# Graph attention layer: other tiles for the transferred sums, group ends on every second step, earlier loads of the row factors, a fifth special tile

## The chip, the cores and the metric

The kernel runs on one core of a Trainium2 chip. The metric is the device time of one execution in microseconds (us). Before the change it is 2991.66 us, the median of 3 runs (2991.22 to 2992.32).

The engines are called as the profile calls them: PE multiplies matrices (PEld loads its weights), DVE is the vector engine, ACT the engine for activations, POOL the general one, SP issues most transfers (DMAs). Each takes its instructions in the order in which the program lists them.

## What is computed

Two layers of a graph network over 4096 nodes with 512 features. Layer 0 is not touched. Layer 1, cut to what matters:

```python
h = jnp.maximum(_layernorm(x, axis=-1), 0.0)
data1 = (h @ W.T + b).reshape(N, H, D)            # N 4096, H 8 heads, D 64
src = jnp.einsum('nhd,xhd->nh', data1, src_proj)
trg = jnp.einsum('nhd,xhd->nh', data1, trg_proj)
e = src.T[:, :, None] + trg.T[:, None, :]
e = jnp.where(e >= 0, e, 0.01 * e)
e = e + adj[None, :, :]
scores = jax.nn.softmax(e, axis=-1)
out = jnp.einsum('hnm,hmd->hnd', scores, data1.transpose(1, 0, 2))
x = x + out.transpose(1, 0, 2).reshape(N, H * D)
```

For every head and every node n, 4096 weights over m are made, summed (the divisor) and used to average the rows of data1.

## The kernel before

Layer 0 takes the first 1760 us or so. Then layer 1 runs in **8 groups**: 4 blocks of 1024 nodes n, times 2 halves of the heads, 4 heads each. In a group there are **32 tiles**, one for each 128 nodes m. A step of the loop at the end of the layer is one tile of one group; 256 steps in all.

One tile of a group holds, for each of the 4 heads k, the unnormalized weights `pr{k}`: 128 nodes m on the partitions, 1024 nodes n along them. It comes about like this:

- `load` (3 steps ahead): SP fetches the tile of the transposed adjacency, `e`, 512 KB (three buffers).
- `exps` (1 ahead): ACT takes exp of it into PSUM, `ex`. `last_exps` (2 ahead): ACT takes exp with a bias, `e3`, for head 3, in which a factor of the row is already contained. `relus` (2 ahead): ACT makes `rl` for head 0 from the row factor `z0`.
- `weigh` (1 ahead): DVE multiplies for each head in the order 3, 0, 1, 2 the larger of a row factor `z{k}` and a column factor by `ex` or `e3` (L756; L753 for head 0). These are four DVE instructions on 128 x 1024 a tile.
- On the **special tiles**, BY_LOG, head 0 goes without DVE: `logs` (5 ahead) has ACT make `lg` from the row term `u` (L731), a transfer issued by POOL adds the adjacency to it on the way (L732), and `relus` takes one exp of the sum (L739).
- `gather` (0 ahead): PE multiplies the weights with the rows of data1 (`pv`, L788). For fp32 the profile shows two instructions for each matmul in the source: 32 a tile. Each writes 32 of the 128 rows of a PSUM tile; the four blocks of 32 rows belong to two **sides**, r = 0 (the first 64 rows) and r = 1.

The divisors are sums over all m of the same weights. Heads 1 and 2 go through PE in each tile (`dn<-pr,d_m`, 8 instructions, all four blocks). Head 3 is added up by POOL (`acc3`, L765) and enters PE once, at the last tile. For **head 0** there are two ways:

- on the tiles of **BY_DMA** a transfer issued by POOL adds the tile to one of two accumulators `acc00` and `acc01` in turn (L770, L772); both enter PE at the last tile;
- on all others, `by_pe`, PE sums the tile itself (`dn<-pr,zo`, L802): 4 instructions on the two blocks of one side. `side` changes with each such tile, and a tile begins its matmuls with the side that is not behind.

Before, BY_DMA is 2, 3, 4, 6, 7, 8, 10, 11, 12, 14, 15, 16, 18, 19, 20, 22, 23, 24, 26 (19 tiles), and by_pe 0, 1, 5, 9, 13, 17, 21, 25, 27, 28, 29, 30, 31 (13 tiles). The special tiles are 17, 21, 25, 29.

The **end of a group**, `finish`, runs inside the next group, one piece behind each step's gather: copy and transposes of the divisors (the small matmuls at L827), their reciprocal `rd`, and then for each of 8 pieces of 128 nodes two transposes on PE (`turn`, L843, 128 x 128, in the trace a pair of instructions of 0.44 us together), four scaled copies on ACT (`o`), for each two pieces an accumulating transfer that adds x1 (POOL, L870) and a store (SP, L873), three calls behind the accumulation. The transposes so lie behind tiles 2 to 9. Group 0 carries no end of a group but `tables`, which makes the row factors of the other groups, with transposes behind tiles 2, 4 and 5.

The **row factors** `z0` to `z3` of the next group (L691) are loaded at tiles 20, 22, 24, 26, `u` at tile 28. There are two sets of buffers for z, used by groups in turn; one for `u`. All loads and stores named "SP" are in one queue, in the order of the program. `finish_last` closes the last group, with ACT and DVE sharing 8 transposed pieces.

At the last tile, dn gets the sums of heads 1 and 2, head 0 of the tile (side 0), head 3 of the tile (side 1), acc01 (side 0), acc00 (side 0) and acc3 (side 1), in this order.

Of the kernel before, what the change touches and what calls it, by code (L numbers as in the profile page):

```python
# [8 lines left out]
FP = mybir.dt.float32  # L9
# [6 lines left out]
P = 128  # L16
# [12 lines left out]
def kernel(  # L29
# [15 lines left out]
    nc = tc.nc  # L45
    N, F = x.shape
    H, D = 8, 64
    HG, WL = 4, 1024
    WT = WL // P
    NT = N // P  # L50
# [49 lines left out]
    with tc.tile_pool(name="w0", bufs=1) as wp, tc.tile_pool(name="a0", bufs=2) as ap_, tc.tile_pool(  # L100
        name="a0s", bufs=8
# [15 lines left out]
        lg = wp.tile([P, NT], FP, name="lg")  # L117
# [514 lines left out]
    HV = WL // BL  # L632
    JT = BL // P
    Q = P // 4
    BY_LOG = (17, 21, 25, 29)
    BY_DMA = [m for m in range(2, NT - 5) if m % 4 != 1]

    with tc.tile_pool(name="p", bufs=2) as prp, tc.tile_pool(name="rl", bufs=2) as rlp, tc.tile_pool(
        name="io1", bufs=3
    ) as iop, tc.tile_pool(name="s1", bufs=1) as sp, tc.tile_pool(name="za", bufs=1) as zp0, tc.tile_pool(name="e3", bufs=2) as e3p, tc.tile_pool(  # L640
        name="zb", bufs=1
    ) as zp1, tc.tile_pool(name="e", bufs=3) as ep, tc.tile_pool(name="ac", bufs=2) as acp, tc.tile_pool(
        name="os", bufs=1
    ) as osp, tc.tile_pool(name="u", bufs=1) as usp, tc.tile_pool(
        name="p_x", bufs=1, space=PSUM
    ) as p_x, tc.tile_pool(name="p_v", bufs=1, space=PSUM) as p_v, tc.tile_pool(
        name="p_t1", bufs=1, space=PSUM
# [9 lines left out]
        def tables():  # L657

            for h in range(H):
                nc.scalar.activation(s_n[:, h, :], s_n[:, h, :], AF.Relu, bias=tmb[:, h:h + 1])  # L660
                if h % 3 == 2:
                    yield
            pz = p_t.tile([P, 2, P], FP, name="pt")
            for g in range(H // HG):
                nc.tensor.transpose(pz[:NT, g, :], s_n[:, g * HG, :], ident)
            yield
            ut = sp.tile([NT, 2, P], FP, name="ut")
            nc.scalar.copy(ut, pz[:NT])
            nc.gpsimd.dma_start(u_d.rearrange("g t p -> t g p"), ut)
            nc.scalar.activation(s_n, s_n, AF.Exp, scale=-(1.0 - SLOPE))  # L670
            yield
            s_f = s_n.rearrange("p h t -> p (h t)")
            for c in range(H * NT // P):
                pz = p_t.tile([P, P], FP, name="pt")
                nc.tensor.transpose(pz, s_f[:, c * P:(c + 1) * P], ident)
                yield
                zt = sp.tile([P, P], FP, name="zt", bufs=2)
                nc.scalar.copy(zt, pz)
                nc.gpsimd.dma_start(z_d[c * P:(c + 1) * P, :], zt)
            yield  # L680
# [12 lines left out]
        def load(i, m):  # L693
            b, g = groups[i]
            e = ep.tile([P, WL], FP, name="e")
            nc.sync.dma_start(e, adj_t[m * P:(m + 1) * P, b * WL:(b + 1) * WL])
            ra[i, m] = e
            if i + 1 < len(groups) and m == 28:
                us[i + 1] = usp.tile([P, WL], FP, name="u")
                b, g = groups[i + 1]  # L700
                nc.sync.dma_start(us[i + 1], row_bcast(u_d, WL, g * N + b * WL))
            if i + 1 < len(groups) and m in (20, 22, 24, 26):
                zload(i + 1, ORDER[(m - 20) // 2])

        def scale(i, m):

# [20 lines left out]
        def logs(i, m):  # L727
            if m in BY_LOG:
                b, g = groups[i]
                r = rlp.tile([P, WL], FP, name="lg", bufs=1)  # L730
                nc.scalar.activation(r, us[i], AF.Relu, bias=nlg_m[:, g, m:m + 1], scale=-(1.0 - SLOPE))  # L731
                nc.gpsimd.dma_start(r, adj_t[m * P:(m + 1) * P, b * WL:(b + 1) * WL], accum_op=ALU.add)  # L732
                rl[i, m] = r
# [40 lines left out]
        def gather(i, m):  # L774
            b, g = groups[i]
            last = m == NT - 1
            if m == 0:
                pv[i] = ([[p_v.tile([P, BL], FP, name=f"pv{c}{q}") for q in range(HV)] for c in range(2)],
                         p_v.tile([P, BL], FP, name="dn"))
            v, dn = pv[i]  # L780
            by_pe = [u for u in range(NT) if u not in BY_DMA]
            side = sum(u < m for u in by_pe) % 2
            for c, pair in enumerate(((3, 0), (1, 2))):
                for q in range(HV):
                    for r in (side, 1 - side):
                        k = pair[r]
                        for c0 in range(0, D, Q):
                            nc.tensor.matmul(v[c][q][r * D + c0:r * D + c0 + Q, :],  # L788
                                             va[:, m, g * HG + k, c0:c0 + Q],
                                             pr[i, m, k][:, q * BL:(q + 1) * BL], start=(m == 0), stop=last)  # L790

            def den(r, w, src, q, **fl):
                nc.tensor.matmul(dn[r * Q:r * Q + w.shape[1], :], w, src[:, q * BL:(q + 1) * BL], **fl)  # L793

            for r in (side, 1 - side):
                for q in range(HV):
                    hk = g * 2 + r
                    den(r * HV + q, d0_m[:, hk, m, :] if m else d0_0[:, hk, :], pr[i, m, r + 1], q,
                        start=(m == 0), stop=False)
            if m in by_pe:  # L800
                for q in range(HV):
                    den(side * HV + q, zo[:, 1 - side:3], pr[i, m, 0], q, start=False, stop=False)  # L802
            if last:
                for q in range(HV):
                    den(HV + q, zo[:, 1:3], pr[i, m, 3], q, start=False, stop=False)
                for q in range(HV):
                    den(q, zo[:, 1:3], acc[i, 0, 1], q, start=False, stop=False)
                for r, a in enumerate((acc[i, 0, 0], acc[i, 3])):
                    for q in range(HV):
                        den(r * HV + q, zo[:, 1:3], a, q, start=False, stop=True)  # L810
            for k in range(HG):
                pr.pop((i, m - 1, k), None)
            if last:
                os_ = [[osp.tile([P, BL], FP, name=f"os{c}{q}") for q in range(HV)] for c in range(2)]
                for c in range(2):
                    for q in range(HV):
                        nc.scalar.copy(os_[c][q], v[c][q])
                late[i] = os_, dn

        def denominators(i):  # L820
            os_, dn = late.pop(i)
            od = osp.tile([P, BL], FP, name="od")
            nc.scalar.copy(od, dn)
            yield os_
            pd = p_t.tile([P, JT, 2, 4], FP, name="pt")
            for j in range(JT):
                nc.tensor.matmul(pd[:, j, :, :].rearrange("p e r -> p (e r)"), od[:, j * P:(j + 1) * P],  # L827
                                 pick.rearrange("p e r -> p (e r)"), start=True, stop=True)
            yield
            rd = sp.tile([P, JT, 2, 4], FP, name="rd")  # L830
            nc.vector.reciprocal(rd, pd)
            yield rd

# [18 lines left out]
        def finish(i):  # L852


            dens = denominators(i)
            os_ = next(dens)
            yield
            next(dens)
            yield
            rd = next(dens)  # L860
            pts, os2 = {}, {}
            for t in range(WT + 4):
                if 0 < t <= WT:
                    if t % 2:
                        o = iop.tile([P, 2, HG, D], FP, name="o")
                    for r, k in enumerate(ORDER):
                        nc.scalar.activation(o[:, (t - 1) % 2, k, :], pts[t - 1][:, r, :], AF.Copy,
                                             scale=share(rd, t - 1, r))
                    if t % 2 == 0:
                        nc.gpsimd.dma_start(o, part(x1, i, t - 2, 2), accum_op=ALU.add)  # L870
                        os2[t] = o
                if t - 3 in os2:
                    nc.sync.dma_start(part(out, i, t - 5, 2), os2[t - 3])  # L873
                if t < WT:
                    pts[t] = p_t.tile([P, HG, D], FP, name="pt")
                    turn(os_, t, pts[t])
                yield

        def finish_last(i):
# [6 lines left out]
            os_ = next(dens)  # L886
            pts = [p_v.tile([P, HG, D], FP, name=f"pv{c}{q}") for q in range(HV) for c in range(2)]
            xs = p_x.tile([P, 4, HG, D], FP, name="ex")
            pts += [xs[:, n, :, :] for n in range(4)]
            for t in range(4):  # L890
                turn(os_, t, pts[t])
            next(dens)
# [64 lines left out]
        factors(0, 1)  # L957
        scale(0, 1)

        stages = ((load, 3), (logs, 5), (exps, 1), (weigh, 1), (factors, 2), (scale, 2), (gather, 0))  # L960
        for s in range(len(steps)):
            for f, ahead in stages:
                if s + ahead < len(steps):
# [4 lines left out]
                ending = finish(s // NT - 1)  # L968
            if s == len(steps) - 2:
                ending = finish_last(len(groups) - 1)  # L970
            next(ending, None)
        for _ in ending:
            pass

# [33 lines left out]
```

## Time and profile before

| What | us |
|---|---|
| median of 3 runs | 2991.66 |
| the profiled execution | 2991.82 |
| its span | 2990.0 |
| start of the first pv of layer 1 | 1763.1 |
| first pv of group 1 | 1918.3 |
| first pv of group 2 | 2070.8 |
| first pv of group 3 | 2221.1 |
| first pv of group 4 | 2373.4 |
| first pv of group 5 | 2523.6 |
| first pv of group 6 | 2675.5 |
| first pv of group 7 | 2825.8 |

The span is the time from the first instruction to the end of the last; the profiled execution is 1.8 us longer than it. The difference between two rows of the table is the length of a group: 155.2, 152.5, 150.2, 152.3, 150.2, 151.9 and 150.2 us.

In rows of the order of time, the columns are the start in us, the duration in us, the engine, the line, the operation, out<-in by the program's names, the form and the number of instructions that are merged; in brackets the idle time of the engine before, and what ended it. A row with x32 covers 32 matmuls that overlap. Rows of waits give who waited, the total in us, how often, and the longest.

### The profile page before, as it was taken

The page shows a single profiled execution, that of the slowest core. Times are in us where ns is not written, and L with a number is a line of the kernel's source. Part 1 is how long each engine was busy: PE and PEld are TensorE (multiplying, and loading weights), DVE is VectorE, ACT ScalarE, POOL GpSimd, SP SyncE. Part 2 cuts the span into 40 slices and gives each one's busy share as a digit, 9 for nine tenths or more (in the row PEclk, how much of TensorE's full clock was granted, in tenths as well). Part 3 has the DMA queues.
Part 4 walks back from the last instruction along what each step waited for, and adds up shares of the span by engine and source line. Part 5 has one row for each costly group of instructions (what it writes and reads, how often), then busy time and mean ns, then how long its engine had stood idle before and what let it go on. Part 6 is the DMA issues. An engine that isn't in the chain of part 4 may idle for free.

```text
span 2990.0 us, 43039 instructions
## 1 busy us (share of the span) xinstructions
PE 2942.8 (98%) x15371; PEld 1155.0 (39%) x15371; DVE 2607.1 (87%) x3596; ACT 1325.5 (44%) x1852; POOL 1340.9 (45%) x1042
## 2 busy tenths in 40 slices
PE   8999999998999999999999989999999999999998
PEld 4444444444344444444444433323222322232222
DVE  5434777778999999998997789999999999999998
ACT  2111111111112122122122368888777777777776
POOL 3401111112333343443443657575757575757574
PEclk9999999999999999999999999999999999999999
DMA  4205666667875674664553239696969696979795
GB/s 155 95 7 185 224 219 223 227 217 181 195 169 153 156 184 149 173 190 144 177 179 110 62 113 226 199 247 198 249 201 242 204 243 208 237 209 237 213 228 156
DMA packets 454055, 552.01 MB, mean 185 GB/s; under 512 B 261624, under 2 KB 287256, under 8 KB 453840
## 3 DMA queue, kind: packets, MB, share of 16 engines
q1 hardware_dynamic: 400816, 387.81, 42.1%
q0 software_dynamic: 51008, 157.51, 22.8%
q10 hardware_dynamic: 2016, 3.93, 0.4%
q8 instruction: 121, 1.98, 0.3%
q14 instruction: 94, 0.77, 0.1%
HBM read 409.47 MB, written 59.97 MB: 157 GB/s over the span
## 4 chain that ended last, share of the span: by engine, by line
PE 76%; DVE 11%; DMA 4%; SPq 3%; issue 3%; ACT 2%; POOL 0%; DVEq 0%; ACTq 0%; POOLq 0%
PE pv L788 22%; PE po L435 18%; PE pe L288 15%; PE dn L793 7%; PE ps L159 4%; PE po L505 4%; PE pe L166 4%; DVE pr L756 4%; SPq L366 3%; DVE mk L392 2%; DMA acc<-pr 2%; DVE at L405 2%; DVE pt L396 1%; DVE pt L378 1%; DMA eb<-e_d 1%
## 5 line engine op out<-in xcount | busy, mean ns | idle before, releaser
L788 PE MATMUL pv<-pr,sup 128*32 128x512 f32 x8192 | 1009.5, 595 | 9.4 <-POOL d_m L953 5.4
L435 PE MATMUL po<-sup,at 128*128 128x512 f32 x2048 | 899.7, 596 | 8.8 <-DVE at L405 6.8
L765 POOL TENSOR_TENSOR acc<-acc,pr 128x1024 f32<-128x1024 f32 x232 | 558.2, 2406 | 316.2 <-DVE pr L756 315.8
L756 DVE SCALAR_TENSOR_TENSOR pr<-z,g_m,ex 128x1024 f32<-128x1024 f32 x512 | 630.6, 1271 | 6.0 <-ACT ex L714 5.8
L435 PEld LDWEIGHTS po<-sup,at 128*128 128x128 f32 x2048 | 383.2, 190 | 504.4 <-issue 435.6
L415 POOL TENSOR_TENSOR racc<-racc,ex 128x512 f32<-128x512 f32 x240 | 323.5, 1348 | 457.9 <-ACT ex L399 455.9
L788 PEld LDWEIGHTS pv<-pr,sup 128*32 128x32 f32 x8192 | 288.6, 110 | 592.3 <-issue 527.4
L399 ACT ACTIVATE ex<-d 128x512 f32<-128x512 f32 x256 | 160.8, 630 | 708.4 <-DVE d L397 699.8
L288 PE MATMUL pe<-he_t,he_t 128*128 128x512 f32 x896 | 386.4, 592 | 0.0
L714 ACT ACTIVATE ex<-e 128x1024 f32<-128x1024 f32 x256 | 263.1, 1028 | 225.1 <-DVE pr L756 224.7
L756 DVE SCALAR_TENSOR_TENSOR pr<-z,g_m,e 128x1024 f32<-128x1024 f32 x256 | 328.2, 1282 | 10.3 <-PE pv L788 5.4
L793 PE MATMUL dn<-pr,d_m 128*2 128x512 f32 x1984 | 335.1, 592 | 0.0
L724 ACT ACTIVATE e<-e,ld_m 128x1024 f32<-128x1024 f32 x256 | 291.0, 1137 | 11.0 <-DMA e<-in_adj_t_dram 10.9
L753 DVE SCALAR_TENSOR_TENSOR pr<-rl,ngd_m,ex 128x1024 f32<-128x1024 f32 x224 | 284.7, 1271 | 1.6 <-ACT ex L714 1.2
L742 ACT ACTIVATE rl<-z,ngd_m,d_m 128x1024 f32<-128x1024 f32 x224 | 275.1, 1228 | 0.0
L288 PEld LDWEIGHTS pe<-he_t,he_t 128*128 128x128 f32 x896 | 169.2, 190 | 210.1 <-issue 190.5
L291 ACT COPY es<-pe 128x512 f32<-128x512 f32 (+2 forms) x144 | 79.2, 550 | 377.1 <-PE pe L288 377.1
L292 POOL DMA_DIRECT2D e_d<-es x144 | 78.6, 546 | 364.6 <-ACT es L291 359.1
L392 DVE TENSOR_SCALAR mk<-a 128x512 f32<-128x512 f32 x256 | 219.3, 857 | 3.8 <-DMA a<-in_adj_t_dram 3.8
L405 DVE TENSOR_TENSOR at<-ex,a 128x512 f32<-128x512 f32 x256 | 193.5, 756 | 13.9 <-ACT ex L399 9.5
L397 DVE TENSOR_TENSOR d<-pt,mk 128x512 f32<-128x512 f32 x256 | 176.9, 691 | 8.9
L293 DVE CUSTOM_DVE_ANT_0 mk<-pe,mk 128x512 f32<-128x512 f32 (+2 forms) x144 | 92.9, 645 | 99.7 <-ACT es L291 99.7
(173 smaller groups left out, 2606.0 us busy)
## 6 DMA issues: line engine op xcount, KB each, us to landing
e<-in_adj_t_dram SPq DMA_DIRECT2D x256, 512.0 KB, 5.6
acc<-pr POOLq DMA_DIRECT2D x152, 512.0 KB, 5.9
a<-in_adj_t_dram SPq DMA_DIRECT2D x256, 256.0 KB, 3.2
ar<-in_adj_dram SPq DMA_DIRECT2D x120, 256.0 KB, 2.9
e_d<-es POOLq DMA_DIRECT2D x120, 256.0 KB, 3.1
eb<-e_d SPq DMA_DIRECT2D x456, 64.0 KB, 2.8
ac<-in_adj_t_dram SPq DMA_DIRECT2D x112, 256.0 KB, 3.5
et<-e_d SPq DMA_DIRECT2D x112, 256.0 KB, 3.3
```

The source lines that it names most:

```text
L288: nc.tensor.matmul(pe[:, :w], he_t[i][:, k, (t % TB) * P:(t % TB + 1) * P], he_t[j][:, k, BL - w:], start=(k == 0), stop=(k == KC - 1))
L392: nc.vector.tensor_scalar(mk, aj[b, m], 0.0, NEG_BIG, ALU.is_le, ALU.mult)
L415: nc.gpsimd.tensor_tensor(racc, racc, e, ALU.add)
L435: nc.tensor.matmul(po[j], w[:, j * P:(j + 1) * P], sup[:, m, :], start=(m == 0), stop=last)
L714: nc.scalar.activation(x_, ra.pop((i, m)), AF.Exp)
L724: nc.scalar.activation(x_, ra[i, m], AF.Exp, bias=ld_m[:, h // HG, m:m + 1])
L742: nc.scalar.activation(r, zs_[i, 0], AF.Relu, bias=ngd_m[:, h // HG, m:m + 1], scale=d_m[:, h, m:m + 1])
L753: nc.vector.scalar_tensor_tensor(w, rl.pop((i, m)), ngd_m[:, h // HG, m:m + 1], x_, op0=ALU.subtract, op1=ALU.mult)
L756: nc.vector.scalar_tensor_tensor(w, zs_[i, k], g_m[:, h + k, m:m + 1], e3.pop((i, m)) if k == 3 else x_, op0=ALU.max, op1=ALU.mult)
L765: nc.gpsimd.tensor_tensor(acc[i, 3], acc[i, 3], w, ALU.add)
L788: nc.tensor.matmul(v[c][q][r * D + c0:r * D + c0 + Q, :], va[:, m, g * HG + k, c0:c0 + Q], pr[i, m, k][:, q * BL:(q + 1) * BL], start=(m = ...
L793: nc.tensor.matmul(dn[r * Q:r * Q + w.shape[1], :], w, src[:, q * BL:(q + 1) * BL], **fl)
```

## The change

Parts of the diff, all in layer 1:

- BY_LOG has five tiles, 15, 19, 22, 25, 28, two buffers (a pool of their own), and `logs` runs 6 steps ahead.
- BY_DMA is 2, 4, 6, 8, 10, 12, 14, 16, 18, 24 and the five special tiles: 15 tiles. So by_pe is 0, 1, 3, 5, 7, 9, 11, 13, 17, 20, 21, 23, 26, 27, 29, 30, 31: 17 tiles.
- from group 1 on, the row factors of the next group are loaded at tiles 4, 6, 8, 10; in group 0 at 20 to 26 as before.
- from group 1 on, a piece of `finish` runs on steps 0, 1, 2 of a group and then on each even step. The transposes so lie behind tiles 2, 4, ... 16. The store follows its accumulation by one call. `o` has two buffers in place of three.
- at the last tile the sum of head 3 of the tile comes ahead of the others.
- the order of the last four transposed pieces in `finish_last`, a buffer more each for `zt` and `rd`, the place of the pool of `u`.

```diff
-    BY_LOG = (17, 21, 25, 29)
-    BY_DMA = [m for m in range(2, NT - 5) if m % 4 != 1]
+    BY_LOG = (15, 19, 22, 25, 28)
+    BY_DMA = sorted({*range(2, NT // 2 + 1, 2), 18, 24, *BY_LOG})
...
-        name="io1", bufs=3
-    ) as iop, tc.tile_pool(name="s1", bufs=1) as sp, tc.tile_pool(name="za", bufs=1) as zp0, tc.tile_pool(name="e3", bufs=2) as e3p, tc.tile_pool(
+        name="io1", bufs=2
+    ) as iop, tc.tile_pool(name="s1", bufs=1) as sp, tc.tile_pool(name="u", bufs=1) as usp, tc.tile_pool(name="za", bufs=1) as zp0, tc.tile_pool(name="e3", bufs=2) as e3p, tc.tile_pool(
...
-    ) as osp, tc.tile_pool(name="u", bufs=1) as usp, tc.tile_pool(
+    ) as osp, tc.tile_pool(name="lg", bufs=2) as lgp, tc.tile_pool(
...
-                zt = sp.tile([P, P], FP, name="zt", bufs=2)
+                zt = sp.tile([P, P], FP, name="zt", bufs=3)
...
-            if i + 1 < len(groups) and m in (20, 22, 24, 26):
-                zload(i + 1, ORDER[(m - 20) // 2])
+            m0 = 4 if i else 20
+            if i + 1 < len(groups) and m in range(m0, m0 + 8, 2):
+                zload(i + 1, ORDER[(m - m0) // 2])
...
-                r = rlp.tile([P, WL], FP, name="lg", bufs=1)
+                r = lgp.tile([P, WL], FP, name="lg")
...
+            if last:
+                for q in range(HV):
+                    den(HV + q, zo[:, 1:3], pr[i, m, 3], q, start=False, stop=False)
             for r in (side, 1 - side):
...
             if last:
-                for q in range(HV):
-                    den(HV + q, zo[:, 1:3], pr[i, m, 3], q, start=False, stop=False)
                 for q in range(HV):
                     den(q, zo[:, 1:3], acc[i, 0, 1], q, start=False, stop=False)
...
-            rd = sp.tile([P, JT, 2, 4], FP, name="rd")
+            rd = sp.tile([P, JT, 2, 4], FP, name="rd", bufs=2)
...
-            for t in range(WT + 4):
+            for t in range(WT + 2):
...
-                if t - 3 in os2:
-                    nc.sync.dma_start(part(out, i, t - 5, 2), os2[t - 3])
+                if t - 1 in os2:
+                    nc.sync.dma_start(part(out, i, t - 3, 2), os2[t - 1])
...
-            pts += [xs[:, n, :, :] for n in range(4)]
+            pts += [xs[:, n, :, :] for n in (0, 2, 1, 3)]
...
-        stages = ((load, 3), (logs, 5), (exps, 1), (weigh, 1), (factors, 2), (scale, 2), (gather, 0))
+        stages = ((load, 3), (logs, 6), (exps, 1), (weigh, 1), (factors, 2), (scale, 2), (gather, 0))
...
-            next(ending, None)
+            if s < NT or s % 2 == 0 or s % NT < 3 or s > len(steps) - 3:
+                next(ending, None)
```

## The prediction

> **What bounds layer 1 now.** I read the page first, for the shares; the chain of waits puts 76% of the span on PE and 11% on DVE, so those two are the candidates.
>
> ```profile
> PE 76%; DVE 11%; DMA 4%; SPq 3%; issue 3%; ACT 2%; POOL 0%; DVEq 0%; ACTq 0%; POOLq 0%
> ...
> L788 PE MATMUL pv<-pr,sup 128*32 128x512 f32 x8192 | 1009.5, 595 | 9.4 <-POOL d_m L953 5.4
> ```
>
> Layer 1 is 8 groups of 32 tiles. I then asked for the busy time of each engine over one group (the columns are PE, PEld, DVE, ACT, POOL, clock, DMA share, GB/s), and for who waits for whom from 2070 to 2826 us, five groups, first on PE and then on DVE.
>
> ```profile
> 2070.00:2221.00 151.00, 151.00 (x1380) 44.53 (x1374) 149.04 (x126) 118.11 (x140) 95.08 (x57) 1.00 0.83 224
> ```
> ```profile
> PE pv L788 <- DVE pr L756: 0.3, 1, 0.3
> ```
> ```profile
> DVE pr L756 <- ACT os L817: 3.8, 5, 1.2
> DVE pr L756 <- PE pv L788: 3.7, 7, 0.7
> ```
>
> Both engines look full: 151.0 and 149.0 of 151 us. The waits separate them: in five groups PE waited for DVE once, 0.3 us, while DVE waited seven times for PE. The order of time on PE shows what a tile costs there. Tile 9 of group 2 starts at 2115.82:
>
> ```profile
> 2111.02 3.64 PE L788 MATMUL pv<-pr,sup 128*32 128x512 f32 x32
> 2114.48 1.04 PE L793 MATMUL dn<-pr,d_m 128*2 128x512 f32 x8
> 2115.45 0.44 PE L843 MATMUL pt<-ident,os 128*128 128x128 f32 x2
> 2115.82 3.64 PE L788 MATMUL pv<-pr,sup 128*32 128x512 f32 x32
> 2119.28 1.04 PE L793 MATMUL dn<-pr,d_m 128*2 128x512 f32 x8
> 2120.14 1.03 PE L793 MATMUL dn<-pr,zo 128*3 128x512 f32 x4
> 2121.09 0.44 PE L843 MATMUL pt<-ident,os 128*128 128x128 f32 x2
> 2121.46 3.64 PE L788 MATMUL pv<-pr,sup 128*32 128x512 f32 x32
> 2124.92 1.04 PE L793 MATMUL dn<-pr,d_m 128*2 128x512 f32 x8
> 2125.78 3.62 PE L788 MATMUL pv<-pr,sup 128*32 128x512 f32 x32
> ```
>
> Start to start of pv: **4.32 us** (4.29 on the tiles after, 2125.78 to 2130.07) for a bare tile, **4.80** with the transposes of a group end (+0.51), **5.64** where the sum of head 0 goes through PE as well (+0.84). The eight dn of d_m take 0.86 (2119.28 to 2120.14); the four dn of zo take as long, since they use only one of the two sides of dn and the other stands still. Call that 0.85 a unit. Two such tiles on opposite sides share a unit if nothing stands between them: tile 13 has side 0 and costs nothing visible (2134.36, 2138.66: 4.30), its dn run beside the next tiles' pv, and tile 17, side 1, pays the one unit (5.14). A transpose uses all 128 columns and ends that. Group 0 shows it one tile later: the sum of tile 1 overlaps the pv of tile 2, and the unit is paid at the transposes behind tile 2, 5.56 us from start to start:
>
> ```profile
> 1777.91 0.59 PE L793 MATMUL dn<-pr,zo 128*3 128x512 f32 x2
> 1777.92 0.60 PE L788 MATMUL pv<-pr,sup 128*32 128x512 f32 x2
> ...
> 1783.16 0.40 PE L665 MATMUL pt<-ident,s_n 128*32 128x128 f32 x2
> 1783.48 3.64 PE L788 MATMUL pv<-pr,sup 128*32 128x512 f32 x32
> ```
>
> The Trainium skill (TensorEngine Tiling, Key Properties) says that tiles run independently and that a change of tiling mode drains the engine. By that rule alone the changes of mode, eight a group before and after, make +0; by the rows above the units that can no longer pair make the difference worked out below.
>
> So a group on PE alone is 32 x 4.29 = 137.3, 8 transposes x 0.51 = 4.1, the four small matmuls of the divisors about 1.1, and 10 units (tiles 5, 9, the pairs 13/17, 21/25, 27/28, 29/30, four at the border with tiles 31, 0, 1 and the accumulators) = 8.5: **151.0**. Measured from the start of group 2 (2070.82) to that of group 7 (2825.76): 755.0 / 5 = 151.0. PE sets the pace of groups 2 to 7, with no waits inside. DVE needs 4.77 for a tile of four products (2099.07 to 2103.84), so 28 x 4.77 + 4 x 3.58 = 147.9 a group: it has 3 us to spare.
>
> **The change, part by part.**
>
> *Sums by transfer on other tiles.* 15 tiles in place of 19, so 17 in place of 13 are summed on PE: 0, 1, 3, 5, 7, 9, 11, 13, 17, 20, 21, 23, 26, 27, 29, 30, 31. With the ends of groups on every second step, transposes follow tiles 2, 4, ... 16. Each of tiles 3, 5, 7, 9, 11, 13 has transposes behind the next tile, before a partner comes: 6 units. Then pairs 17/20, 21/23, 26/27, 29/30: 4 units. Ten inside the group where there were six; the border keeps its four. **+4 x 0.85 = +3.4 a group**, on the engine that sets the pace. Bounds: if skew did survive the transposes, 14 tiles would pair to 7 units, against five if the ten of before did too, or six as measured: +0.85 to +3.4. I take the upper end, as group 0's row is this very case.
>
> *Four transfers fewer* for the sums: 4 x 0.87 us of issue on POOL, which stands idle 316 us before its accumulations; they land in 5.9 us, on no one's path in groups 2 to 7. Worth 0.
>
> *A fifth special tile.* Its product moves from DVE to ACT: -1.19 on DVE (4.77 / 4), +1.07 on ACT (relu with u 1.15 and exp 1.15 for relu with z 1.23), which is busy 118 of 151. One more accumulating transfer of 512 KB, 9.8 us to landing; four tiles lie between its issue and its use (three before), 17 us. Two buffers: tile 22's is that of tile 15, long read. ACT waited up to 1.9 us for the pr0 buffer of special tiles (7.2 us in five groups); a late ACT makes DVE's next ex late, and DVE is 1.4 to 3.2 us ahead of PE at tiles 2 to 11. 0 in groups 2 to 7.
>
> *Row factors at tiles 4 to 10.* Four loads of 512 KB, about 1.2 us of issue each on SP, go in front of the e loads of tiles 5, 7, 9, 11 instead of 21, 23, 25, 27. They land in 6.6 to 11.6 us. The stretch they go to has the DMA engines at 0.68 (2081 to 2101), and 0.99 to 1.03 was measured at tiles 11 to 16. Their buffers were last read one group earlier. Behind them wait e loads, behind these ACT, then DVE's lead: 0.
>
> *Group ends on every second step, store one call after the accumulation in place of three.* Same 8 transposes, 32 copies, 4 + 4 transfers. SP now reaches a store one tile sooner (two tiles behind the accumulation, not three). It already waits for it 17 times of 28, 19.6 us in all, so expect some 5 us each time, with the next e load behind it. That load has two DVE periods, 2 x 4.77, from the release of its buffer to its use by ACT and lands in 5.7: some 4 us to spare. An accumulation is issued about 5 us behind the release that SP waits for before the store and lands in 6.3, so at 11.3; the next e load could go at 2 x 4.77 + 1.0 = 10.6. So 0.7 us and the issue of the store, 0.6, are used of the 4. 0; if the cover fails, 28 stores x up to 1 us.
>
> *pr3's sum first at the last tile, order of the last transposes, more zt and rd, other places in SBUF.* Same matmuls at the border, 4 units either way: 0, with up to one unit per border either way (7 x 0.85 = 6). In the last transposes ACT and DVE took turns from 2981.95 to 2986.13; side by side DVE alone would need 2.9 us: 0 to -1.2, and I take 0, as DVE waited for ACT across both halves of ex alike. Shifted places may move the first loads of the layer; the longest wait there was 5.4 us (d_m), which they do not feed: -1 to +1, 0 taken.
>
> *Groups 0 and 1.* Here DVE does pace PE: tiles 14 to 16 of group 0 start 4.77 apart with 0.27 waits for pr. One product less gives DVE 1.2 us back; PE's own sum for its tiles 1 to 31 becomes 143.6 (31 x 4.29, 1.2 transposes, 9 units, 1.7 at the border) against 144.7 measured: **-1.1**. Group 1 took 152.5 as it began behind; it becomes 151.0 + 3.4: **+1.9**.
>
> Sum: -1.1 + 1.9 + 6 x 3.4 = **+21.2** on the profiled span of 2990.0, so 3011.2; that execution's own time was 2991.8, 1.8 more, and the median of the runs 2991.7, the same within 0.2. I say 3013 us.
>
> **Rivals.**
> 1. *DVE is the bound.* The Trainium skill (Perfetto Trace Analysis, Identifying the Most-Contended Engine) takes the occupancy of the vector engine as a fair measure and calls PE's busy share a bad one; by it the 99% of DVE would be the limit. On the rows alone: if DVE paced every group, one product less each saves 8 x 1.19 = 9.5, **2982**. For it: DVE is idle 0 to 2 us a group. Against: its idle time ends with PE, and PE starts are 4.29 apart where DVE needs 4.77. It decides only if PE's extra units cost under 1.2 us a group.
> 2. *The units pair after all:* +0.85 to +1.7 x 7 groups, less 1: **2997 to 3003**; with the gains of groups 0 and 1 fuller, no change.
> 3. *The stores block SP* and e comes late: 28 x 0.4 to 1 us on top, **3024 or more**. For it: 17 waits now. Against: the 4 us to spare and a slower PE, which gives everyone else time.
>
> **How the numbers follow.** A change of 0.2% (6 us) is about what can be told from none here. My forecast (units in full): 0.70. Rival 1: 0.10. Rival 2: 0.14, of which 0.06 is within 0.2%. Rival 3: 0.06. Slower 0.84, same 0.06, faster 0.10. The forecast's own range is 3005 to 3021 (border units and start, 6 + 2 either way); with rival 2 and the nearer half of rival 3 it is 2996 to 3026.
>
> **What would show it.** In groups 2 to 7 pv starts 5.64 apart at tiles 4, 6, ... 14 and 4.29 at 3, 5, ... 13; groups 154.4 us apart; DVE idle some 5 us a group, waiting for PE; 120 acc and 40 lg transfers. Wrong if tiles 4 to 14 take 4.80, if PE waits for pr or DMA inside a group, or if the groups come closer than 151 us.

## The result, and the profile after

The changed kernel takes **3013.85 us**, the median of 4 runs (3012.7 to 3015.76); the kernel before, beside it, 2991.44 (2989.87 to 2992.32). The ratio is 1.0076, with a 95% interval of 1.0059 to 1.0094: slower by 22 us. The profiled span is 3010.9 against 2990.0, 20.9 more; the prediction worked out 21.2 on the span and 3013 us in all.

Where the time went can be read from the starts of the first pv of each group:

| Piece | before, us | after, us | difference | predicted |
|---|---|---|---|---|
| start of layer 1 | 1763.1 | 1761.4 | -1.7 | 0 |
| group 0 | 155.2 | 155.0 | -0.2 | -1.1 |
| group 1 | 152.5 | 155.0 | +2.5 | +1.9 |
| groups 2 to 6 | 754.9 | 772.1 | +17.2 | +17.0 |
| group 7, to the start of its last tile | 145.0 | 148.4 | +3.4 | +3.4 |
| from there to the end | 19.2 | 18.9 | -0.3 | 0 |

Groups 2 to 6 take 154.4 us each, without exception. The order of time on PE of the changed kernel, from tile 2 of group 2 on (start, duration, engine, line, operation, tiles, form, number):

```profile
2082.83 3.64 PE L791 MATMUL pv<-pr,sup 128*32 128x512 f32 x32
2086.29 1.04 PE L796 MATMUL dn<-pr,d_m 128*2 128x512 f32 x8
2087.26 0.44 PE L847 MATMUL pt<-ident,os 128*128 128x128 f32 x2
2087.63 3.64 PE L791 MATMUL pv<-pr,sup 128*32 128x512 f32 x32
2091.09 1.04 PE L796 MATMUL dn<-pr,d_m 128*2 128x512 f32 x8
2091.95 0.60 PE L796 MATMUL dn<-pr,zo 128*2 128x512 f32 x2
2091.96 0.60 PE L791 MATMUL pv<-pr,sup 128*32 128x512 f32 x2
...
2095.82 1.45 PE L796 MATMUL dn<-pr,d_m 128*2 128x512 f32 x6
2097.20 0.44 PE L847 MATMUL pt<-ident,os 128*128 128x128 f32 x2
2097.57 3.64 PE L791 MATMUL pv<-pr,sup 128*32 128x512 f32 x32
```

Tile 3 begins at 2087.63. Its sum of head 0 (zo) does not hold up tile 4: the first pv of tile 4 stands beside it at 2091.96, 4.33 us after the start of tile 3. The price comes at the transposes behind tile 4, which begin only after the last sums of the side that is late (the row at 2095.82, then 2097.20): tile 5 starts at 2097.57, 5.61 us after tile 4. Tile 2, with transposes and nothing behind, took 4.80. So a lone sum costs 0.81 to 0.85 one tile later, exactly where the next transposes are, and the pattern 4.33, 5.61 repeats up to tile 14.

The waits on DVE and on ACT in the changed kernel, five groups from 2071 to 2844 us (who waited, total us, how often, longest), and the busy times of the first of them (PE, PEld, DVE, ACT, POOL, clock, DMA share, GB/s); PE has no wait at all in this stretch:

```profile
DVE pr L759 <- PE dn L796: 9.7, 10, 1.2
DVE pr L759 <- ACT os L821: 5.3, 5, 1.3
DVE pr L759 <- PE pv L791: 4.8, 25, 0.2
DVE pr L756 <- ACT ex L717: 4.2, 11, 0.6
```
```profile
ACT pr L742 <- DMA acc<-pr: 5.4, 5, 2.5
...
ACT e L727 <- DMA e<-in_adj_t_dram: 0.4, 2, 0.2
```
```profile
2071.00:2225.00 154.00, 154.00 (x1388) 44.77 (x1382) 148.62 (x125) 117.38 (x140) 92.66 (x54) 1.00 0.79 209
```

DVE is now idle some 5 us a group where it was idle 2; PE is the first reason, as expected, but not the only one. ACT hardly ever waits for the adjacency any more (6.9 us before). What DVE was relieved of and the quieter transfers (DMA share 0.79, before 0.83) went into idle time.

### The profile page after: what moved, and what is told of

Read it like the earlier page. It is cut to its first block, busy times and chain, and to the rows that moved or that the text cites. A ratio compares the mean times of both kernels' runs of the same rounds, so it can differ in the third digit from the quotient of the medians.

```text
span 3010.9 us, 43191 instructions
## 1 busy us (share of the span) xinstructions
PE 2965.1 (98%) x15499; PEld 1151.3 (38%) x15499; DVE 2608.4 (87%) x3588; ACT 1328.8 (44%) x1860; POOL 1320.9 (44%) x1018
## 5 line engine op out<-in xcount | busy, mean ns | idle before, releaser
L791 PE MATMUL pv<-pr,sup 128*32 128x512 f32 x8192 | 1031.8, 594 | 7.4 <-POOL d_m L957 5.5
L796 PE MATMUL dn<-pr,d_m 128*2 128x512 f32 x1984 | 360.0, 592 | 0.0
L756 DVE SCALAR_TENSOR_TENSOR pr<-rl,ngd_m,ex 128x1024 f32<-128x1024 f32 x216 | 275.2, 1274 | 11.6 <-ACT ex L717 11.3
L745 ACT ACTIVATE rl<-z,ngd_m,d_m 128x1024 f32<-128x1024 f32 x216 | 265.3, 1228 | 0.0
```

The source lines that it names most:

```text
L745: nc.scalar.activation(r, zs_[i, 0], AF.Relu, bias=ngd_m[:, h // HG, m:m + 1], scale=d_m[:, h, m:m + 1])
L756: nc.vector.scalar_tensor_tensor(w, rl.pop((i, m)), ngd_m[:, h // HG, m:m + 1], x_, op0=ALU.subtract, op1=ALU.mult)
L791: nc.tensor.matmul(v[c][q][r * D + c0:r * D + c0 + Q, :], va[:, m, g * HG + k, c0:c0 + Q], pr[i, m, k][:, q * BL:(q + 1) * BL], start=(m = ...
```

## The experiments

Each run is the changed kernel or the one before with the lines shown. "Before" of the ratios is the kernel before on the same chip (2992.55 us beside experiments 1, 2, 4 and the first run of 6; 2991.65 beside 5, 7 and the first run of 8; 2992.52 beside 3 and the second runs of 6 and 8). The runs of a kernel lie some 1 to 3 us to either side of their median, those of experiments 4, 5, 6 and 8 up to 7.

**1. The sums alone.** The old kernel with the new list:

```diff
-    BY_DMA = [m for m in range(2, NT - 5) if m % 4 != 1]
+    BY_DMA = [2, 4, 6, 8, 10, 12, 14, 15, 16, 18, 19, 22, 24, 25, 28]
```

> The kernel before with the new list of transferred tiles alone (15 tiles); four special tiles, ends of groups on each step and late row factors as before. Theory of units: transposes now stand behind tiles 2 to 9, so tiles 3, 5, 7, 9 cost a unit each and 11/13 pair, then four pairs: 9 units inside a group against 6, +2.55 us a group, +15 in groups 2 to 7 and +1 to +2 in groups 0 and 1: 3007 to 3010. Rival, the ends of groups or the loads carry the loss: below 3000. Rival DVE: with 28 products on DVE as before the time is that of before, 2989 to 2993.

Measured 3008.4 us, as forecast, ratio 1.0053 (1.0038 to 1.0068), +15.9 over the median of before. Groups 2 to 6 take 153.6 us, which is 151.0 plus three units. The list alone carries most of the loss, and DVE, with 28 products as before, follows. The order of time on PE in this run, tiles 3 to 5 of group 2:

```profile
2088.53 3.64 PE L788 MATMUL pv<-pr,sup 128*32 128x512 f32 x32
2091.98 1.04 PE L793 MATMUL dn<-pr,d_m 128*2 128x512 f32 x8
2092.84 1.03 PE L793 MATMUL dn<-pr,zo 128*2 128x512 f32 x4
2093.80 0.44 PE L843 MATMUL pt<-ident,os 128*128 128x128 f32 x2
2094.17 3.64 PE L788 MATMUL pv<-pr,sup 128*32 128x512 f32 x32
2097.62 1.04 PE L793 MATMUL dn<-pr,d_m 128*2 128x512 f32 x8
2098.60 0.44 PE L843 MATMUL pt<-ident,os 128*128 128x128 f32 x2
2098.97 3.64 PE L788 MATMUL pv<-pr,sup 128*32 128x512 f32 x32
```

5.64 with the sum, 4.80 without. The changed kernel lies 5.5 us above this run: its ends on every second step stretch the transposes to tile 16, and the pair 11/13, which shares a unit here (5.14 at tile 13), is parted too. One unit in seven groups is 6.0.

**2. One product more on DVE.** The changed kernel with tile 28 no longer special, its transfer kept:

```diff
-    BY_LOG = (15, 19, 22, 25, 28)
-    BY_DMA = sorted({*range(2, NT // 2 + 1, 2), 18, 24, *BY_LOG})
+    BY_LOG = (15, 19, 22, 25)
+    BY_DMA = sorted({*range(2, NT // 2 + 1, 2), 18, 24, 15, 19, 22, 25, 28})
```

> The changed kernel with tile 28 no longer special (15, 19, 22, 25 are), the transferred tiles unchanged: DVE gets one product a group back. Theory of units: DVE has some 5 us a group to spare, so nothing in groups 1 to 7 and up to +1 in group 0: 3013 to 3016. Rival DVE: 8 x 1.19 = +9.5, 3022 to 3024.

Measured 3014.24 us, ratio 1.0073 (1.0056 to 1.0089); groups 2 to 6 at 154.4 as in the changed kernel. Eight products of 1.19 us on an engine that is busy 149 of 154 us cost nothing that can be measured. DVE isn't the bound of the changed kernel.

**3. The moved loads and the store, each put back.** The changed kernel with late row factors, and with the store two calls behind:

```diff
-            m0 = 4 if i else 20
+            m0 = 20
```
```diff
-            for t in range(WT + 2):
+            for t in range(WT + 3):
...
-                if t - 1 in os2:
-                    nc.sync.dma_start(part(out, i, t - 3, 2), os2[t - 1])
+                if t - 2 in os2:
+                    nc.sync.dma_start(part(out, i, t - 4, 2), os2[t - 2])
```

> The changed kernel with the row factors at tiles 20 to 26 again, nothing else. The prediction's term of 0 for the move: 3012 to 3016. Rival, the early loads are what keeps the later tiles free of DMA waits: 3020 or more, with PE starts off their pattern at tiles 20 to 31. Rival, the early loads cost: below 3010.

> The changed kernel with the store two calls behind its accumulation in place of one. The prediction's term of 0 for the store: 3012 to 3016, though SP's wait for it (139.6 us in the changed kernel) falls to under 30 us. Rival, the waiting store costs here as it does with the block of transfers: 3005 or less.

Measured 3015.85 (1.0063 to 1.0093) and 3015.95 (1.0061 to 1.0095): no difference to 3013.85 that can be told, as the kernel before, beside them, lay 1.1 us higher too. Late row factors bring ACT 15.7 us of waits for e in five groups, and groups 2 to 6 still average 154.4. The store's wait in the changed kernel is large, and goes unnoticed. SP's own waits, changed kernel, 2071 to 2844 us:

```profile
SPq L698 <- ACT ex L717: 579.3, 149, 5.3
SPq L877 <- DMA o<-x: 98.0, 20, 7.7
```

That is 4.9 us for each store, and the e loads behind it still come in time. With the store two calls behind, SP does not wait for it at all, and the time is the same.

**4. The same number of sums, in one block.** The forecast's own test: 15 transfers at tiles 2 to 16, so 17 sums at 0, 1 and 17 to 31, all inner ones in pairs.

```diff
-    BY_DMA = sorted({*range(2, NT // 2 + 1, 2), 18, 24, *BY_LOG})
+    BY_DMA = list(range(2, 17))
```

> The changed kernel with the 15 transferred tiles as one block, 2 to 16, and so the 17 tiles summed on PE as 0, 1 and 17 to 31: same number of sums on PE and same number of transfers, only no lone sum ahead of transposes. Theory of units: tiles 17 to 30 make 7 pairs, 7 units inside a group in place of 10, so a group of 154.4 us becomes 151.9; 7 x 2.55 = 18 us less than the changed kernel, 2995 to 2997, and tiles 4 to 14 take 4.80 with transposes and 4.3 without. Rival, it is the number of sums on PE that costs, wherever they are: 3012 to 3015. Rival, transfers on neighbouring tiles beside the early row factors hold up pr0: above 3000, with DVE waiting for a DMA.

Measured **3054.6 us**, ratio 1.0207 (1.0192 to 1.0222), 41 us above the changed kernel where 18 below was forecast. The units went as forecast: tiles 4, 6, 8 take 4.77 in place of 5.61, and the sums from 17 on pair up (4.33 and 5.14 in turn). But at the transposes behind tiles 10 and 14 PE stood still. Group 2, PE, then ACT, then SP:

```profile
2150.96 1.04 PE L796 MATMUL dn<-pr,d_m 128*2 128x512 f32 x8
2156.37 0.44 PE L847 MATMUL pt<-ident,os 128*128 128x128 f32 x2 [4.37 <-ACT o L871]
2156.74 5.34 PE L791 MATMUL pv<-pr,sup 128*32 128x512 f32 x32
```
```profile
2153.23 1.15 ACT L727 ACTIVATE e<-e,ld_m 128x1024 f32<-128x1024 f32 x1 [4.12 <-DMA e<-in_adj_t_dram]
2154.28 1.23 ACT L745 ACTIVATE rl<-z,ngd_m,d_m 128x1024 f32<-128x1024 f32 x1
2155.41 0.90 ACT L871 ACTIVATE o<-pt,rd 128x64 f32<-128x64 f32 x4
```
```profile
2121.84 13.13 SPq L698 DMA_DIRECT2D e<-in_adj_t_dram  x4
2143.34 0.40 SPq L877 DMA_DIRECT2D out_dram<-o  x1
2143.84 13.75 SPq L698 DMA_DIRECT2D e<-in_adj_t_dram  x4
```

Read from the bottom: SP issues no e load between 2135 and 2143.84, while the store waits 8.3 us for its accumulation. The e load after it comes late, ACT waits 4.12 us for it, and since ACT works in order, the copies `o` of a group end wait behind; the transposes on PE wait for these 4.37 us. The busy times of the stretch (PE, PEld, DVE, ACT, POOL, clock, DMA share, GB/s):

```profile
2100.00:2115.00 15.00, 15.00 (x140) 4.32 (x136) 15.00 (x14) 11.97 (x19) 11.48 (x8) 1.00 1.01 270
2115.00:2130.00 15.00, 15.00 (x142) 4.37 (x138) 14.91 (x13) 9.70 (x13) 11.02 (x8) 1.00 1.01 221
2130.00:2145.00 15.00, 12.97 (x121) 3.60 (x116) 13.02 (x12) 12.85 (x19) 10.23 (x9) 1.00 1.07 253
2145.00:2160.00 15.00, 10.63 (x90) 2.95 (x86) 10.64 (x10) 9.36 (x13) 9.42 (x7) 0.91 1.04 251
```

The DMA engines are full for 60 us on end. In the changed kernel they stand at 0.76, 0.92 and 0.78 in the three 15 us from 2092 to 2137, and are full only after that, at 1.04 and 1.00 from 2137 to 2172. So the late accumulation goes with full DMA engines; that they alone make it late isn't shown (experiments 6 and 7).

Behind its wait PE is slower too: the pv at 2156.74 take 5.34 us in place of 3.64, with a granted clock of 0.72 from 2156.7 to 2162.7. In groups 2 to 6 the transposes wait 29.1 us for ACT's copies, and one tile in each group is slow in this way, by 1.7 us. Together that is 37.5 of the 38.6 us that these groups lie above their units (798.1 against 5 x 151.9).

**5. Is it the store, or the loads?** The block once more, with the store two calls behind (the edit of experiment 3), and with late row factors.

> The block of transfers at 2 to 16 once more, with the store two calls (four tiles) behind its accumulation in place of one call (two tiles). Theory A, the store waits at the head of SP's queue for an accumulation that full DMA engines make late, and the e loads behind it come late: without that wait 2996 to 3002, and ACT waits for e under 5 us in groups 2 to 6 (39 before). Theory B, the DMA engines are simply full with 15 transfers in a row beside the row factors: above 3030, with e late all the same.

> The block of transfers at 2 to 16 with the row factors at tiles 20 to 26 as in the kernel before, the store one call behind as changed. Theory B, DMA engines full: four loads of 512 KB less between tiles 4 and 16 bring it to 2996 to 3005. Theory A, the store's wait: it stays above 3020, with the store waiting 100 us or more in groups 2 to 6.

Measured 3031.42 (1.0108 to 1.0141) and 3059.77 (1.0206 to 1.0239). The farther store takes 23 us off: in five groups ACT's waits for e fall from 39.4 to 15.7 us, and PE's waits at the transposes from 29.1 to 15.3. Late row factors, beside the near store, take nothing off. So of some 58 us that the block lies above its units (2996), two fifths are the store at the head of SP's queue. Each theory holds in one run and misses in the other: theory B's number for the first (above 3030) and theory A's for the second (above 3020, the store waiting 124 us) came true, and neither cause alone explains both.

The cause of the other 35 us stays open. The transfers of the sums land late, in 8.3 us (median) against 5.7 in the changed kernel. But full DMA engines alone don't explain it: in the second run of experiment 6, with the same frame and the same store, the sums land in 7.7 us, the DMA share is 0.96 to 1.08 from 2107 to 2197, and groups 2 to 6 stay within 0.6 us of their units. The traces show one thing more. In the block DVE loses its lead: in group 2 the first product of tile 3 starts 7.8 us before the first pv of that tile, that of tile 14 only 4.5 (7.8 and 7.1 in the changed kernel), since two tiles take PE 4.32 + 4.77 there and DVE 2 x 4.77. With a smaller lead a late e reaches PE sooner; no run separates this from the late transfers.

**6. The old sums in the new frame.** The changed kernel with the 19 tiles of before, with the store one and two calls behind:

```diff
-    BY_DMA = sorted({*range(2, NT // 2 + 1, 2), 18, 24, *BY_LOG})
+    BY_DMA = [m for m in range(2, NT - 5) if m % 4 != 1]
```

> The changed kernel with the old list of transferred tiles (19 tiles), everything else as changed. Theory of units: lone sums at 5, 9, 13 and pairs 17/21, 25/27, 28/29, with 30 carried into the border: 10 units a group with the border, as before, so groups 2 to 7 take 151.0; with DVE relieved in groups 0 and 1 and the layer starting 1.7 us earlier, 2986 to 2990. Rival, the other parts cost time of their own: above 2992. Rival DVE, every group shorter by 1.2: 2980 to 2983.

> The changed kernel with the old list of 19 transferred tiles and the store two calls behind. By the units this program is the kernel before on PE, 151.0 a group, and yet it took 3007.6 with the store one call behind. Theory A, the waiting store delays e while the DMA engines are full at tiles 10 to 24: 2987 to 2996, with the stretches of 7 to 8 us at tile 14 gone. Theory B, the density of transfers at tiles 10 to 24 alone: 3003 or more.

Measured 3007.6 (1.0033 to 1.0063) and 2996.82 (1.0006 to 1.0025). The first one missed its forecast of 2986 to 2990: ACT waited 21.6 us for e, the store 141.1. With the store farther these are 1.6 and none, and the time lies 0.8 us above theory A's range:

```profile
SPq L698 <- ACT ex L717: 658.3, 161, 5.8
SPq L693 <- DVE pr L756: 10.8, 11, 1.0
SPq L698 <- DMA e<-in_adj_t_dram: 0.4, 2, 0.2
```

Groups 2 to 6 come to 151.0 to 151.6; the units say 151.0. What is left above before lies in groups 0 and 1 (158.4 and 153.3, against 155.2 and 152.5). So the near store costs 11 us with 19 transfers, 23 with the block, and nothing that can be told with the changed kernel's 15 (experiment 3).

**7. The lone sums taken out.** The kernel before with tiles 5 and 9 by transfer too:

```diff
-    BY_DMA = [m for m in range(2, NT - 5) if m % 4 != 1]
+    BY_DMA = [m for m in range(2, NT - 5) if m % 4 != 1 or m < 13]
```

> The kernel before with tiles 5 and 9 summed by transfer too (21 transfers), nothing else: the two lone sums ahead of transposes go. Theory of units: 8 units a group in place of 10, 149.3 us, which DVE's 147.9 of products and its short waits just allow: 150.2 to 149.3 a group, 2978 to 2987. Rival DVE: no gain, 2989 to 2993. Rival DMA, two more transfers fill the queue at tiles 2 to 12: 2995 or more.

Measured **2982.61 us** (6 runs, 2980.48 to 2984.76), as forecast, ratio 0.9968 (0.9956 to 0.9979): **faster than both**, by 9 us than the kernel before, with fewer units and no other edit. Tile 5 of group 2, which took 5.64 before:

```profile
2094.43 3.64 PE L788 MATMUL pv<-pr,sup 128*32 128x512 f32 x32
2097.88 1.04 PE L793 MATMUL dn<-pr,d_m 128*2 128x512 f32 x8
2098.86 0.44 PE L843 MATMUL pt<-ident,os 128*128 128x128 f32 x2
2099.22 3.64 PE L788 MATMUL pv<-pr,sup 128*32 128x512 f32 x32
```

Tiles 2 to 9 all take 4.80, and groups 2 to 6 149.3 to 150.5. Two of the five (149.3 and 149.5) come to the units' 149.3; DVE's 4.77 a tile shows at tiles 22 to 28 of the groups, where PE waits for it five times, 1.2 us in all. The DMA engines are as full here as in the block: their share is 1.00 to 1.08 from 2090 to 2190. So full engines alone don't cost time; here the ends of groups lie at tiles 2 to 9 and the store three calls behind.

**8. Two ways to go on from there.** A fifth special tile, 13, and early row factors:

```diff
-    BY_LOG = (17, 21, 25, 29)
+    BY_LOG = (13, 17, 21, 25, 29)
```
```diff
-            if i + 1 < len(groups) and m in (20, 22, 24, 26):
-                zload(i + 1, ORDER[(m - 20) // 2])
+            m0 = 4 if i else 20
+            if i + 1 < len(groups) and m in range(m0, m0 + 8, 2):
+                zload(i + 1, ORDER[(m - m0) // 2])
```

> As the run before it, with tile 13 special as well (five special tiles, one buffer, 13, 17, 21, 25, 29): DVE 1.19 us a group shorter, PE the same. Theory of units: groups 2 to 7 at 149.3 in full, groups 0 and 1 gain 1 to 2 more: 2974 to 2981, below the run without it by 2 to 6. Rival, PE alone counts and DVE is nowhere near: no difference to it. Rival DMA: the fifth accumulating transfer makes e late, slower than it.

> The kernel before with tiles 5 and 9 by transfer (2982.6) and the row factors of the next group at tiles 4 to 10 from group 1 on. Theory: what is left above 149.3 a group there are DMA waits of ACT at tiles 21 to 31, beside the row factors; loaded early, the groups come to 149.3: 2975 to 2980. Rival, the early stretch fills up, e comes late at tiles 6 to 14: 2985 or more. Rival, DVE is what is left: no change, 2981 to 2984.

Measured 3000.0 (1.0019 to 1.0038) and 2990.77 (0.9982 to 1.0001). Both are worse than 2982.61 and miss their forecasts of 2974 to 2981 and 2975 to 2980. The special tile has ACT write pr0 (three buffers) while the transfers still read it; on ACT, in group 2:

```profile
2131.49 1.15 ACT L739 ACTIVATE pr<-lg,t_m 128x1024 f32<-128x1024 f32 x1 [3.25 <-DMA acc<-pr]
2132.67 1.15 ACT L731 ACTIVATE lg<-u,nlg_m 128x1024 f32<-128x1024 f32 x1
2133.72 1.01 ACT L714 ACTIVATE ex<-e 128x1024 f32<-128x1024 f32 x1
```

ACT stands 3.25 us for pr0, and ex for DVE comes behind it; such waits add up to 21.8 us in five groups (6.4 without the tile). Tile 13 of that group takes 5.98 us, and the three after it DVE's 4.8.

With early row factors ACT waits 3.10 us for e at tile 9 of group 2:

```profile
2118.76 1.15 ACT L725 ACTIVATE e<-e,ld_m 128x1024 f32<-128x1024 f32 x1 [3.10 <-DMA e<-in_adj_t_dram]
```

Tile 9 takes 6.0 to 6.3 in groups 2 to 4 and 4.80 in groups 5 to 7; ACT's waits for e are 18.3 us in five groups (7.0 without). That is the rival of that run, with its number. Its reason, that the stretch fills up, isn't shown: the DMA share from 2110 to 2130 is 1.08 with the early loads and without them.

## Why the prediction was right

**The pace.** That PE sets it in groups 2 to 7, in spite of DVE's 99%, held: PE waited for no one there, and a product given back to DVE cost nothing (3014.24). The Trainium skill takes the vector engine's occupancy for a fair measure (Perfetto Trace Analysis, Identifying the Most-Contended Engine). The measurement decides against it here: a kernel at DVE's pace would have come to 2982 (rival 1). It is the waits, and the distances from start to start, that told the two full engines apart.

**The units.** Ten inside a group where there were six: forecast 154.4 us, measured 154.4. Tiles 4, 6, ... 14 were forecast at 5.64 and came at 5.61, the odd ones at 4.29 and came at 4.33. The row of group 0 that this rested on, one lone sum paid a tile later at the transposes, is the picture that all seven groups now show. Rival 2 (the units pair after all) is refuted by the same rows.

The ten units of before, border included, are a mean. Its groups take 150.2 and 151.9 to 152.3 us in turn, mainly because one unit of the border falls now to the one group and now to the other: a last tile of 6.02 is followed by tiles of 4.32 and 7.06, one of 6.85 by 4.29 and 6.25, 17.4 us either way. In the changed kernel it is always the first, and so its groups are equal.

One reading in the prediction was wrong. The transposes in group 0's row have the form 128*32: they use 32 columns, not 128. So the rows show that a transpose ends the pairing, and at what price, 0.81 to 0.85 us; that its width is the reason isn't shown. The Trainium skill's rule that a change of mode drains the engine (TensorEngine Tiling, Key Properties) fits these rows, but no row shows the mode.

**The terms of 0.** The fifth special tile, the moved row factors and the nearer store are each 0 within the 1 or 2 us that the runs can tell, shown one by one. The store's wait was forecast at some 5 us each and measured at 5.0 (28 stores, 139.6 us); e did not come late for it (0.4 us in five groups). That the place in SBUF and the order at the last tile cost nothing was only argued. The layer's start, 1.7 us earlier, isn't their doing as far as the runs show: it lay between 1761.4 and 1764.4 in all profiles, whichever places they had.

**Groups 0 and 1** were mis-sized by 0.9 and 0.6 us. DVE did stop holding up PE in group 0, as forecast (from its tile 14 on five waits of PE for products, 1.4 us in all, before; none after). But group 0 pays one unit of its border more: its last tile takes 6.83, where later groups take 6.02, and in return the second tile of group 1 takes 6.24 in place of 7.06. What group 1 has on top is its first tile, 5.70 in place of 4.32: PE waits 1.16 us in it for ACT's copy of the divisors, 0.3 before. The earlier start of the layer hides this in the total; part of the closeness of 3013 to 3013.85 is luck.

**What the terms of 0 did not say.** They hold for this list only. "Four transfers fewer: worth 0" was read off the kernel before; in the frame of the changed kernel with its near store, the same four transfers cost 11 us (experiment 6). Rival 3 had the right mechanism at the wrong place: with 19 transfers the store costs 11 us, with 15 in a row 23. As far as the runs show, the change so keeps its near store harmless with sums on PE that cost more: 3.4 us a group, 24 in seven.

## What to carry to other kernels

Where narrow matmuls on two halves of the array run beside each other, count what each half owes when the next transpose comes; here work for one half was free only if its partner arrived before that. When two engines are both 99% busy, look at who waits for whom and take the distance from start to start before you shift work from one to the other. And a transfer that is off the path at one place in the program can be on it at another. Price it with the waits at the head of its queue and with the lead of the engine that uses it; the DMA share alone didn't tell here (1.0 and more in the fastest run and in the slowest).

## What was not expected of the hardware

With 15 accumulating transfers of 512 KB in neighbouring tiles the DMA share stood at 1.01 to 1.07 for 60 us, and the transfers of o landed late enough to hold SP's queue up to 9.5 us; the loss, some 58 us over its units, is larger than that of the four units a group that the change adds (3.4 us a group, 24 in seven). Moving four loads of 512 KB out of that stretch didn't help (3059.77 against 3054.6, intervals that overlap), while moving only the place of the wait in SP's queue took 23 us off. And a wait of PE costs more than itself: after 4.37 us of it the granted clock was 0.72, and the next tile took 6.0 us in place of 4.3.
